# Queries and keys of a head pair: seven half-depth products per two blocks in place of eight

## The chip, the cores and the metric

The kernel runs on one core of one Trainium2 chip. A core has five engines that run side by side, each through its own list of instructions in order: TensorE (matrix products), VectorE and ScalarE (elementwise work), GpSimd, and SyncE, which here issues most of the transfers. The products are written to a small accumulator memory, PSUM, which the kernel divides into banks of 128 x 512 float32; VectorE and ScalarE move results from there to the main on-chip memory, SBUF. The metric is the time of one execution on the device in microseconds; lower is better.

## The reference, cut to what matters

The whole program is four layers on an image x of 512 channels and 64 x 64 pixels: attention, two gated convolution layers and a linear attention, each added to x. The change lies in the first layer. There x is normalized in groups of channels (subtract a mean, multiply by `rstd`, both per group), and then:

```
q = to_tokens(_conv1x1(fmap, wq, gain_in))
k = to_tokens(_conv1x1(fmap, wk, gain_in))
v = to_tokens(_conv1x1(fmap, wv, gain_in))
AA = jnp.sum(q * q, axis=-1)
qk = jnp.einsum('bid,bjd->bij', q, k)
sim = -(AA[:, :, None] + AA[:, None, :] - 2.0 * qk) * scale
attn = jax.nn.softmax(sim, axis=-1)
out = jnp.einsum('bij,bjd->bid', attn, v)
```

There are 8 heads of 64 channels over 4096 pixels. Everything is float32. `_conv1x1` is a product of a 512 x 512 matrix with the 512 x 4096 image.

## The kernel before, in words

The image stays on the chip as `X`: 128 partitions, NC = 4 chunks of channels, N = 4096 pixels, which are cut into NB = 8 blocks of BLK = 512. `_attention_pairs` (from L383) works on two heads at a time, so there are four pairs. For each pair `project` computes the queries Q (kept in the tile `O` of the pair), the keys K, the values V with pixels on the partitions, and the row sums A of the squared queries. Then, for each of the eight query blocks, a loop over 32 key tiles t makes scores (L502), their exponentials on ScalarE (L510, tile `pt`), the running sum of the exponentials on VectorE (L591, L593, tile `acc`), and the product with the values (L520) two tiles later. `close` sums `acc` over the partitions with two small products `ps_d` (L529), takes the reciprocal (L533) and multiplies (L534); the two lines after that (L535, L538) keep a mark of whether the sums were in range. In a pair, `close` of a block is called inside the next block's loop; that of the last block stands before the `project` of the next pair.

`project` first loads the three weight matrices of the pair in one transfer (L438, tile `wqkv`) and multiplies each by `rstd` (`_Centered.scaled`, L357 on ScalarE and L360 on VectorE or GpSimd). In the first pair `_Centered.take` (L349) also subtracts the mean from x block by block on ScalarE while the products run; for later pairs x is already centred, and the weights are loaded and scaled hundreds of microseconds ahead. Then come eight blocks. Each has four products of 128 x 128 by 128 x 512 for Q and four for K (L457), which accumulate the four chunks in a bank, and sixteen products of 128 x 128 by 128 x 128 for V (L468). Q leaves the bank through ScalarE with its scale (L461) and is squared there (L464); K and V leave through VectorE with theirs (L463, L475). After the last block sixteen small products with `halves` (L483) put the sums of squares in one tile `ps_a`, which VectorE turns (L491) and copies into `A` (L492). The exponentials of the pair wait for `A`.

PSUM is divided between the pool `ps_s`, three tiles of two banks, and the two tiles `av0` and `av1` of the values product. In SBUF the pools that matter are `pt` (five tiles of 128 x 1024), `acc` (two tiles of the same size) and `row` (three tiles of 128 x 512, used by `avs` and `rd` when a block closes).

Nobody writes the order of instructions on an engine by hand here, except in the later layers, where `keep_in_program_order` pins TensorE. A planner simulates the program with costs of its own, places each instruction on its engine's list when its operands and a free tile should be ready, and inserts the waits. The order is then fixed: an instruction that waits holds up all that stands behind it on that engine.

The class `_Seven`, further down in the file, is used by the two later layers already. It computes two output matrices (a and b) for two blocks at once. Each matrix is cut in two halves of depth (two chunks each), and the two by two by two half products, which would be eight, are formed as seven products of sums and differences: `sums` makes four combinations of the weights, `differences` four of the blocks, and `steps` holds the seven products p1 to p7 with the additions of their results.

Of the kernel before, what the change touches and what calls it, by code (L numbers as in the profile page):

```python
# [10 lines left out]
FP = mybir.dt.float32  # L11
AF = mybir.ActivationFunctionType
ALU = mybir.AluOpType
# [3 lines left out]
P = 128  # L17
# [46 lines left out]
class _Form:  # L64
# [8 lines left out]
    def __init__(self, run, parts, phy, phx, jy, jx, by, bx, oy, ox):  # L73
        self.run = run
        self.parts, self.phy, self.phx, self.jy, self.jx, self.by, self.bx, self.oy, self.ox = (
            parts, phy, phx, jy, jx, by, bx, oy, ox,
        )
        self.planes = phy * phx
        self.ch = 32 // self.planes
        self.rows, self.w = H // phy, W // phx  # L80
        self.part = self.rows // parts
        self.fh, self.fw = self.rows + jy * by - 1, self.w + jx * bx - 1
        self.plane = self.fh * self.fw
        self.n = self.part * self.w
        self.rounds = BLK // self.n
        self.nr = 16 // self.ch
# [289 lines left out]
            )  # L376

SUM_LOW, SUM_HIGH = 1e-20, 1e30  # L380


def _attention_pairs(tc, a, X, QO, gmask, small, centered, stats, okay):  # L383
# [19 lines left out]
    with tc.tile_pool(name="att1", bufs=1) as p1, tc.tile_pool(  # L403
# [29 lines left out]
        V = p1.tile([P, NT, P], FP, tag="V", name="V")  # L433
        A = p1.tile([P, NT, 2], FP, tag="A", name="A")

        def project(pair):
            w = p1.tile([P, 3, NC, P], FP, tag="wqkv", name=f"wqkv{pair}")
            nc.sync.dma_start(out=w, in_=a["L0_wqkv"][pair])  # L438
            for n in range(3):
                centered.scaled(  # L440
                    w[:, n], rstd, nc.gpsimd if pair else nc.scalar if n else nc.vector
                )
            if pair == 0:
                centered.began()
            Q = QO[pair]
            sq = []
            for b in range(NB):
                cols = ts(b, BLK)
                if pair == 0 and b:
                    for c in range(NC):  # L450
                        centered.take(X[:, c, cols], c)
                if b % 2 == 0:
                    sq.append(ptp.tile([P, 2 * BLK], FP, tag="pt", name="sq"))
                for n in range(2):
                    ps = ps_s.tile([P, 2 * BLK], FP, tag="s", name="ps_qk")[:, 0:BLK]
                    for c in range(NC):
                        nc.tensor.matmul(  # L457
                            ps, w[:, n, c, :], X[:, c, cols], start=(c == 0), stop=(c == NC - 1)
                        )
                    if n == 0:  # L460
                        nc.scalar.activation(Q[:, cols], ps, AF.Copy, scale=2 * scale * gain_in)  # L461
                    else:
                        nc.vector.tensor_scalar(K[:, cols], ps, gain_in, None, ALU.mult)  # L463
                nc.scalar.activation(sq[-1][:, ts(b % 2, BLK)], Q[:, cols], AF.Square)  # L464
                ps = ps_s.tile([P, 2 * BLK], FP, tag="s", name="ps_v")[:, 0:BLK]
                for i in range(QT):
                    for c in range(NC):
                        nc.tensor.matmul(  # L468
                            ps[:, ts(i, P)],
                            X[:, c, ts(b * QT + i, P)],  # L470
                            w[:, 2, c, :],
                            start=(c == 0),
                            stop=(c == NC - 1),
                        )
# [4 lines left out]
            psa = ps_s.tile([P, 2 * BLK], FP, tag="s", name="ps_a")  # L479
            for i in range(4):  # L480
                squares = sq[i].rearrange("p (t j k) -> p j t k", j=4, k=32)
                for j in range(4):
                    nc.tensor.matmul(  # L483
                        psa[ts(j, 32), ts(i, 256)].rearrange("p (t k) -> p t k", k=32),
                        halves,
                        squares[:, j],
                        start=True,
                        stop=True,
                    )
            at = ptp.tile([P, 2 * BLK], FP, tag="pt", name="at")  # L490
            nc.vector.transpose(at, psa)  # L491
            nc.vector.tensor_copy(A, at.rearrange("p (t k) -> p t k", k=32)[:, :, 0:2])  # L492
# [167 lines left out]
class _PlaneConv:  # L660
# [58 lines left out]
    def put(self, i, k, ps, more, bias, step):  # L719


        nc = self.nc
        if more is None:
            self.take(i, k, [ps], lambda d, x: nc.scalar.activation(d, x, AF.Identity, bias=bias))
            return

        def fill(d, x, y):
            if step is None:
                nc.vector.tensor_add(d, x, y)
                return  # L730
            for n in range(self.pair):
                nc.vector.scalar_tensor_tensor(  # L732
                    d[:, n], x[:, n], step, y[:, n], ALU.add, ALU.add
                )

        self.take(i, k, [ps, more], fill)
# [97 lines left out]
                yield  # L834


class _Seven:

    def __init__(self, tc, matmul):
        self.nc, self.matmul = tc.nc, matmul

    def sums(self, eng, a, b, s):

        for out, x, y, op in (
            (s[0], b[:, 0:2], b[:, 2:4], ALU.add),
            (s[1], s[0], a[:, 0:2], ALU.subtract),
            (s[2], a[:, 0:2], b[:, 0:2], ALU.subtract),
            (s[3], a[:, 2:4], s[1], ALU.subtract),
        ):
            eng.tensor_tensor(out, x, y, op)
        return s

    def differences(self, eng, x, t):  # L860

        for j, (a, b) in enumerate(
            (
                (lambda c: x(c, 1), lambda c: x(c, 0)),
                (lambda c: x(2 + c, 1), lambda c: t[0][c]),
                (lambda c: x(2 + c, 1), lambda c: x(c, 1)),
                (lambda c: x(2 + c, 0), lambda c: t[1][c]),
            )
        ):
            for c in range(2):  # L870
                yield eng.tensor_tensor(t[j][c], a(c), b(c), ALU.subtract)

    def steps(self, a, b, s, t, x, bank, keep, put):

        nc = self.nc
        ps, kept = {}, {}

        def add(j, w, hs, first):  # L880

            if first:
                ps[j] = bank(j)
            for c in range(2):
                self.matmul(
                    ps[j], w[:, c], hs[c], start=(first and c == 0), stop=(c == 1),
                    skip_group_check=not first,
                )

        def p1():  # L890
            add(0, a[:, 0:2], [x(c, 0) for c in range(2)], True)
            kept[0] = keep(0, ps[0])

        def p5():
            add(1, s[0], t[0], True)
            kept[1] = keep(1, ps[1])

        def p2():
            add(0, a[:, 2:4], [x(2 + c, 0) for c in range(2)], False)
            put(0, 0, ps[0], None)  # L900

        def p7():
            add(2, s[2], t[2], True)
            nc.vector.tensor_add(kept[1], kept[1], ps[2])

        def p6():
            add(3, s[1], t[1], True)
            nc.vector.tensor_add(kept[0], kept[0], ps[3])

        def p3():  # L910
            add(1, s[3], [x(2 + c, 1) for c in range(2)], False)
            put(0, 1, ps[1], kept[0])

        def p4():
            add(2, b[:, 2:4], t[3], False)
            put(1, 0, ps[2], kept[0])
            put(1, 1, kept[1], kept[0])

        return [p1, p5, p2, p7, p6, p3, p4]


@with_exitstack
def _gated_convs(ctx, tc, a, X, vcol, vall, gmask, small, new_stats, centered, stats, F):

# [12 lines left out]
    for layer in ("L1", "L2"):  # L937
# [65 lines left out]
        def summed(i):  # L1003
            t = [w2p.tile([P, NC, P], FP, tag="w", name="w_sum") for _ in range(2)]
            t = [t[n // 2][:, n % 2 * 2 : n % 2 * 2 + 2] for n in range(4)]
            wsum[i] = seven.sums(nc.vector, w_in[i], w_in[i + 1], t)

        def view(k):
            return lambda c, n: pc.pixels(X[:, c, :], 2 * k + n)
# [149 lines left out]
def _linear_attention(ctx, tc, a, X, vcol, vall, ident, gmask, small, centered, stats, F, Z, out):  # L1159
# [55 lines left out]
    with ExitStack() as st:  # L1215
# [78 lines left out]
        def summed(i):  # L1294
            ss = [kvp.tile([P, BLK], FP, tag="kv", name="w_sum") for _ in range(2)]
            ss = [
                t.rearrange("p (n c m) -> p n c m", n=2, c=2)[:, n] for t in ss for n in range(2)
            ]
            wsum[i] = seven.sums(nc.vector, w_qkv[i], w_qkv[i + 1], ss)

        def differences(k, eng):

# [22 lines left out]
        def bank(j):  # L1325
            return ps_vk.tile([P, BLK], FP, tag=f"vk{j}", name="ps7")
# [191 lines left out]
        def steps(hf, q):  # L1518
            return list(blks[hf, q][2])
# [214 lines left out]
```

## Time and profile before

| what | value |
|---|---|
| three runs | 3900.72, 3907.03, 3908.17 us; median 3907.03 us |
| the profiled execution | 3899.94 us, with a span of 3898.2 us from first to last instruction |
| mean granted TensorE clock of it | 0.995 of full speed |
| attention layer in the span | up to about 2295 us |
| TensorE busy | 3811.4 us, 98% of the span |
| VectorE busy, ScalarE busy | 2509.6 us (64%), 2017.3 us (52%) |
| Q and K products (L457) | 512 rows, 227.2 us busy |
| V products (L468) | 1024 rows, 119.5 us busy |

A row of the groups of instructions reads: line, engine, operation, output<-inputs, tile sizes, number, then busy time and mean nanoseconds of one, then the idle time of the engine before them and what ended it. A row of the timeline reads: start, duration, engine, line, operation, and in brackets an idle time before it. Products on TensorE overlap in their start and end, so their durations can't be added; their starts can be compared. A float32 product of the program is two rows of the trace.

### The profile page before, as it was taken

The page shows a single profiled execution, that of the slowest core. Times are in us where ns is not written, and L with a number is a line of the kernel's source. Part 1 is how long each engine was busy: PE and PEld are TensorE (multiplying, and loading weights), DVE is VectorE, ACT ScalarE, POOL GpSimd, SP SyncE. Part 2 cuts the span into 40 slices and gives each one's busy share as a digit, 9 for nine tenths or more (in the row PEclk, how much of TensorE's full clock was granted, in tenths as well). Part 3 has the DMA queues.
Part 4 walks back from the last instruction along what each step waited for, and adds up shares of the span by engine and source line. Part 5 has one row for each costly group of instructions (what it writes and reads, how often), then busy time and mean ns, then how long its engine had stood idle before and what let it go on. Part 6 is the DMA issues. An engine that isn't in the chain of part 4 may idle for free. (4 is left out here: it accounts for less than half of the span.)

```text
span 3898.2 us, 81595 instructions
## 1 busy us (share of the span) xinstructions
PE 3811.4 (98%) x35526; PEld 1692.3 (43%) x35526; DVE 2509.6 (64%) x2944; ACT 2017.3 (52%) x2909; POOL 109.3 (3%) x94
## 2 busy tenths in 40 slices
PE   6999999999999999999999989999999999999999
PEld 4533335333354333353333335554454544455544
DVE  3577772777736777627776755766657767565435
ACT  3577762777735777626665645552255532354210
POOL 0000000000000000000000000000000000121110
PEclk9999999999999999999999999999999999999999
DMA  2000000000000000000000025562055621463334
GB/s 98 9 2 1 1 1 9 1 1 1 1 1 9 1 1 1 1 9 1 1 1 1 1 73 174 177 191 70 36 172 174 189 66 44 149 174 99 94 93 142
DMA packets 194010, 221.55 MB, mean 57 GB/s; under 512 B 13400, under 2 KB 138584, under 8 KB 193520
## 3 DMA queue, kind: packets, MB, share of 16 engines
q1 hardware_dynamic: 166832, 157.12, 14.5%
q10 hardware_dynamic: 26784, 59.11, 4.1%
q8 instruction: 281, 4.60, 0.5%
q14 instruction: 81, 0.66, 0.1%
q0 software_dynamic: 32, 0.06, 0.0%
HBM read 156.46 MB, written 59.77 MB: 55 GB/s over the span
## 5 line engine op out<-in xcount | busy, mean ns | idle before, releaser
L510 ACT ACTIVATE pt<-ps_s,A 128x512 f32<-128x512 f32 x2048 | 1284.5, 686 | 556.6 <-PE ps_s L502 528.9
L593 DVE TENSOR_TENSOR acc<-acc,pt 128x1024 f32<-128x1024 f32 x960 | 1175.6, 1225 | 331.6 <-ACT pt L510 305.8
L520 PE MATMUL av<-pt,V 64*64 64x512 f32 x8192 | 1112.3, 590 | 0.9 <-ACT pt L510 0.9
L502 PE MATMUL ps_s<-O,K 64*64 64x512 f32 x8192 | 1111.4, 589 | 0.0
L520 PEld LDWEIGHTS av<-pt,V 64*64 64x64 f32 x8192 | 339.6, 133 | 557.5 <-issue 525.7
L502 PEld LDWEIGHTS ps_s<-O,K 64*64 64x64 f32 x8192 | 334.1, 133 | 554.2 <-issue 308.7
L765 ACT COPY S<-S 32x1295 f32<-32x1295 f32 (+1 forms) x272 | 341.3, 1256 | 212.0 <-DMA S<-F 131.8
L687 PEld LDWEIGHTS ps_cv<-S,T 64*32 64x32 f32 x13824 | 191.9, 105 | 109.8 <-issue 72.5
L687 PE MATMUL ps_cv<-S,T 64*32 64x128 f32 x13824 | 230.2, 272 | 4.5 <-DVE S L763 1.8
L687 PE MATMUL ps<-h,w_out_L 128*128 128x512 f32 x512 | 228.7, 599 | 1.5 <-DVE X L1087 1.4
L457 PE MATMUL ps_qk<-X,wqkv 128*128 128x512 f32 x512 | 227.2, 597 | 2.8 <-ACT wqkv L357 2.8
L687 PE MATMUL ps<-diff,w_sum 128*128 128x512 f32 x420 | 197.4, 602 | 0.5 <-issue 0.5
L349 ACT ACTIVATE X<-X,gn_less 128x512 f32<-128x512 f32 x120 | 76.8, 709 | 221.9 <-DVE gn_less L102 210.8
L687 PE MATMUL ps<-X,w_in_L 128*128 128x512 f32 x320 | 152.6, 617 | 12.9 <-ACT kept L1017 5.3
L461 ACT ACTIVATE O<-ps_qk 128x512 f32<-128x512 f32 x32 | 19.1, 596 | 258.2 <-PE ps_qk L457 258.2
L1075 DVE SCALAR_TENSOR_TENSOR h<-ps,vec,h 128x512 f32<-128x512 f32 x112 | 82.5, 748 | 105.7 <-PE ps L687 104.2
L687 PEld LDWEIGHTS ps<-h,w_out_L 128*128 128x128 f32 x512 | 94.3, 190 | 120.2 <-issue 98.7
L687 PE MATMUL ps<-h,pw_L 128*128 128x512 f32 x320 | 144.2, 600 | 1.3 <-DVE plane L732 1.2
L457 PEld LDWEIGHTS ps_qk<-X,wqkv 128*128 128x128 f32 x512 | 95.5, 192 | 113.5 <-issue 109.7
L463 DVE TENSOR_SCALAR K<-ps_qk 128x512 f32<-128x512 f32 x32 | 22.1, 692 | 186.9 <-PE ps_qk L457 186.9
L819 DVE STREAM_TRANSPOSE h<-ps_cv 128x512 f32<-128x512 f32 x112 | 109.4, 1050 | 43.5 <-PE ps_cv L687 42.8
L468 PEld LDWEIGHTS ps_v<-wqkv,X 128*128 128x128 f32 x1024 | 119.4, 192 | 15.3 <-issue 15.3
(161 smaller groups left out, 3074.8 us busy)
## 6 DMA issues: line engine op xcount, KB each, us to landing
T<-in_L_T_dram SPq DMA_DIRECT2D x112, 384.0 KB, 3.7
F<-plane ACTq DMA_DIRECT2D x112, 324.0 KB, 2.9
S<-F SPq DMA_DIRECT2D x224, 162.0 KB, 4.3
row<-G SPq DMA_DIRECT2D x80, 272.0 KB, 3.5
S<-G SPq DMA_DIRECT2D x96, 153.0 KB, 4.3
G<-plane ACTq DMA_DIRECT2D x48, 289.0 KB, 2.2
T<-in_L_T_dram SPq DMA_DIRECT2D x48, 256.0 KB, 3.7
out_dram<-y SPq DMA_DIRECT2D x32, 256.0 KB, 2.0
```

Source lines behind the costliest of these rows:

```text
L349: self.nc.scalar.activation(xs, xs, AF.Identity, bias=less)
L457: nc.tensor.matmul(ps, w[:, n, c, :], X[:, c, cols], start=(c == 0), stop=(c == NC - 1))
L463: nc.vector.tensor_scalar(K[:, cols], ps, gain_in, None, ALU.mult)
L468: nc.tensor.matmul(ps[:, ts(i, P)], X[:, c, ts(b * QT + i, P)], w[:, 2, c, :], start=(c == 0), stop=(c == NC - 1),)
L502: nc.tensor.matmul(ps[ts(half, D), ts(h, BLK)], K[rows, t * P + half * D : t * P + (half + 1) * D], QO[pair][rows, cols], start=True, stop ...
L510: nc.scalar.activation(pt[:, ts(h, BLK)], ps[:, ts(h, BLK)], AF.Exp, bias=A[:, t, h : h + 1])
L520: nc.tensor.matmul(av[half][rows, :], V[keys, t, rows], pt[keys, ts(h, BLK)], start=(t == 0), stop=(t == NT - 1),)
L593: nc.vector.tensor_add(acc, acc, pt)
L687: self.tc.keep_in_program_order(self.nc.tensor.matmul(*args, **kw))
L765: nc.scalar.copy(second, first)
L819: nc.vector.transpose(out, src)
L1075: nc.vector.scalar_tensor_tensor(d, ps, bias, d, ALU.add, ALU.mult)
```

## The change

`_Seven` moves ahead of the attention code, and `sums` becomes a generator that yields after each of its four instructions; the two later layers run it to its end in one go, as they did. `project` uses it for Q (matrix a) and K (matrix b), two blocks k = 0 to 3 at a time.

The scales of Q, K and V, which the evictions applied, go into the weights: a small tile `gains` holds `rstd` times the scale of Q and `rstd` times that of K and V, and `scaled` multiplies the weights by it. Evictions become plain copies and additions. V leaves through ScalarE now. The products p1 and p5 start banks 0 and 1 (`av0`, `av1`), p7 and p6 start banks 2 and 3 (tiles of `ps_s`), and p2, p3, p4 accumulate on top. `keep` copies p1 and p5 to tiles of `row` before that.

The four weight combinations lie in one tile of the pool `acc`, the differences in three tiles of `pt` and one of `acc`, made on VectorE. `ps_a` is allocated at the start of `project`, and the row-sum products of two blocks (`squares`) are called after the first V products of the next two.

```diff
+        gains = p1.tile([P, 2, NC], FP, tag="gains", name="gains")
+        nc.vector.tensor_scalar(gains[:, 0], rstd, 2 * scale * gain_in, None, ALU.mult)
+        nc.vector.tensor_scalar(gains[:, 1], rstd, gain_in, None, ALU.mult)
+        seven = _Seven(tc, nc.tensor.matmul)
...
             for n in range(3):
                 centered.scaled(
-                    w[:, n], rstd, nc.gpsimd if pair else nc.scalar if n else nc.vector
+                    w[:, n], gains[:, min(n, 1)],
+                    nc.gpsimd if pair else nc.scalar if n else nc.vector,
                 )
...
-                for n in range(2):
-                    ps = ps_s.tile([P, 2 * BLK], FP, tag="s", name="ps_qk")[:, 0:BLK]
-                    for c in range(NC):
-                        nc.tensor.matmul(
-                            ps, w[:, n, c, :], X[:, c, cols], start=(c == 0), stop=(c == NC - 1)
-                        )
-                    if n == 0:
-                        nc.scalar.activation(Q[:, cols], ps, AF.Copy, scale=2 * scale * gain_in)
-                    else:
-                        nc.vector.tensor_scalar(K[:, cols], ps, gain_in, None, ALU.mult)
-                nc.scalar.activation(sq[-1][:, ts(b % 2, BLK)], Q[:, cols], AF.Square)
+            psa = ps_s.tile([P, 2 * BLK], FP, tag="s", name="ps_a")
+            wsum = p2.tile([P, 2 * BLK], FP, tag="acc", name="w_sum").rearrange(
+                "p (n c m) -> p n c m", n=4, c=2
+            )
+            wsum = [wsum[:, n] for n in range(4)]
+            sums = seven.sums(nc.vector, w[:, 0], w[:, 1], wsum)
+
+            def differences(k):
+                tiles = [ptp.tile([P, 2 * BLK], FP, tag="pt", name="diff") for _ in range(3)]
+                tiles.append(p2.tile([P, 2 * BLK], FP, tag="acc", name="diff"))
+                t = [[t[:, ts(c, BLK)] for c in range(2)] for t in tiles]
+                return t, seven.differences(
+                    nc.vector, lambda c, n: X[:, c, ts(2 * k + n, BLK)], t
+                )
...
-                nc.vector.tensor_scalar(
-                    V[:, ts(b, QT), :].rearrange("p t d -> p (t d)"), ps, gain_in, None, ALU.mult
-                )
+                nc.scalar.copy(V[:, ts(b, QT), :].rearrange("p t d -> p (t d)"), ps)
+
+            def bank(j):
+                if j < 2:
+                    return ps_av.tile([P, BLK], FP, tag=f"av{j}", name="ps7")
+                return ps_mm.tile([P, BLK], FP, tag="mm", name="ps7")
+
+            def keep(j, ps):
+                t = p3.tile([P, BLK], FP, tag="row", name="kept")
+                nc.scalar.copy(t, ps)
+                return t
...
+                def put(m, n, ps, more):
+                    dst = (K if m else Q)[:, ts(2 * k + n, BLK)]
+                    if more is None:
+                        nc.scalar.copy(dst, ps)
+                    else:
+                        nc.vector.tensor_add(dst, ps, more)
...
+                value(2 * k)
+                if k:
+                    late.pop(0)()
+                for _ in range(4):
+                    next(sums, None)
+                    next(pieces)
+                    next(pieces)
+                for step in steps[:5]:
+                    step()
+                value(2 * k + 1)
+                for step in steps[5:]:
+                    step()
+                sq = ptp.tile([P, 2 * BLK], FP, tag="pt", name="sq")
+                for n in range(2):
+                    nc.scalar.activation(
+                        sq[:, ts(n, BLK)], Q[:, ts(2 * k + n, BLK)], AF.Square
+                    )
+                late.append(lambda k=k, sq=sq: squares(k, sq))
```

The seven products and the additions that they call, unchanged but for their place in the file:

```
        def p1():
            add(0, a[:, 0:2], [x(c, 0) for c in range(2)], True)
            kept[0] = keep(0, ps[0])
        def p5():
            add(1, s[0], t[0], True)
            kept[1] = keep(1, ps[1])
        def p2():
            add(0, a[:, 2:4], [x(2 + c, 0) for c in range(2)], False)
            put(0, 0, ps[0], None)
        def p7():
            add(2, s[2], t[2], True)
            nc.vector.tensor_add(kept[1], kept[1], ps[2])
        def p6():
            add(3, s[1], t[1], True)
            nc.vector.tensor_add(kept[0], kept[0], ps[3])
        def p3():
            add(1, s[3], [x(2 + c, 1) for c in range(2)], False)
            put(0, 1, ps[1], kept[0])
        def p4():
            add(2, b[:, 2:4], t[3], False)
            put(1, 0, ps[2], kept[0])
            put(1, 1, kept[1], kept[0])
        return [p1, p5, p2, p7, p6, p3, p4]
```

More of the change, by code (lines that the diff above doesn't have):

```diff
@@ L376, in _normalize, with __init__, sums, differences @@
             )
+class _Seven:
+    def __init__(self, tc, matmul):
+        self.nc, self.matmul = tc.nc, matmul
+    def sums(self, eng, a, b, s):
+        for out, x, y, op in (
+            (s[0], b[:, 0:2], b[:, 2:4], ALU.add),
+            (s[1], s[0], a[:, 0:2], ALU.subtract),
+            (s[2], a[:, 0:2], b[:, 0:2], ALU.subtract),
+            (s[3], a[:, 2:4], s[1], ALU.subtract),
+        ):
+            yield eng.tensor_tensor(out, x, y, op)
+    def differences(self, eng, x, t):
+        for j, (a, b) in enumerate(
+            (
+                (lambda c: x(c, 1), lambda c: x(c, 0)),
+                (lambda c: x(2 + c, 1), lambda c: t[0][c]),
+                (lambda c: x(2 + c, 1), lambda c: x(c, 1)),
+                (lambda c: x(2 + c, 0), lambda c: t[1][c]),
+            )
+        ):
+            for c in range(2):
+                yield eng.tensor_tensor(t[j][c], a(c), b(c), ALU.subtract)
+    def steps(self, a, b, s, t, x, bank, keep, put):
+        nc = self.nc
+        ps, kept = {}, {}
+        def add(j, w, hs, first):
+            if first:
+                ps[j] = bank(j)
+            for c in range(2):
+                self.matmul(
+                    ps[j], w[:, c], hs[c], start=(first and c == 0), stop=(c == 1),
+                    skip_group_check=not first,
+                )
+        def p1():
+            add(0, a[:, 0:2], [x(c, 0) for c in range(2)], True)
+            kept[0] = keep(0, ps[0])
+        def p5():
+            add(1, s[0], t[0], True)
+            kept[1] = keep(1, ps[1])
+        def p2():
+            add(0, a[:, 2:4], [x(2 + c, 0) for c in range(2)], False)
+            put(0, 0, ps[0], None)
+        def p7():
+            add(2, s[2], t[2], True)
+            nc.vector.tensor_add(kept[1], kept[1], ps[2])
+        def p6():
+            add(3, s[1], t[1], True)
+            nc.vector.tensor_add(kept[0], kept[0], ps[3])
+        def p3():
+            add(1, s[3], [x(2 + c, 1) for c in range(2)], False)
+            put(0, 1, ps[1], kept[0])
+        def p4():
+            add(2, b[:, 2:4], t[3], False)
+            put(1, 0, ps[2], kept[0])
+            put(1, 1, kept[1], kept[0])
+        return [p1, p5, p2, p7, p6, p3, p4]
 SUM_LOW, SUM_HIGH = 1e-20, 1e30
@@ L445, in project, with value @@
             Q = QO[pair]
[L446 to L449, printed above, removed]
-                    for c in range(NC):
-                        centered.take(X[:, c, cols], c)
-                if b % 2 == 0:
-                    sq.append(ptp.tile([P, 2 * BLK], FP, tag="pt", name="sq"))
-                for n in range(2):
-                    ps = ps_s.tile([P, 2 * BLK], FP, tag="s", name="ps_qk")[:, 0:BLK]
-                    for c in range(NC):
-                        nc.tensor.matmul(
-                            ps, w[:, n, c, :], X[:, c, cols], start=(c == 0), stop=(c == NC - 1)
-                        )
-                    if n == 0:
-                        nc.scalar.activation(Q[:, cols], ps, AF.Copy, scale=2 * scale * gain_in)
-                    else:
-                        nc.vector.tensor_scalar(K[:, cols], ps, gain_in, None, ALU.mult)
-                nc.scalar.activation(sq[-1][:, ts(b % 2, BLK)], Q[:, cols], AF.Square)
+            psa = ps_s.tile([P, 2 * BLK], FP, tag="s", name="ps_a")
[10 more added lines that the diff above has]
+                    nc.vector, lambda c, n: X[:, c, ts(2 * k + n, BLK)], t
+                )
+            def value(b):
                 ps = ps_s.tile([P, 2 * BLK], FP, tag="s", name="ps_v")[:, 0:BLK]
@@ L474, in project, with squares @@
                         )
[L475 to L481 removed]
+                nc.scalar.copy(V[:, ts(b, QT), :].rearrange("p t d -> p (t d)"), ps)
[7 more added lines that the diff above has]
+                return t
+            def squares(k, sq):
+                sq = sq.rearrange("p (t j k) -> p j t k", j=4, k=32)
                 for j in range(4):
                     nc.tensor.matmul(
[L484 removed]
+                        psa[ts(j, 32), ts(k, 256)].rearrange("p (t k) -> p t k", k=32),
                         halves,
[L486 removed]
+                        sq[:, j],
                         start=True,
@@ L489, in project @@
                     )
+            late = []
+            for k in range(NB // 2):
+                if pair == 0:
+                    for b in (2 * k, 2 * k + 1):
+                        for c in range(NC if b else 0):
+                            centered.take(X[:, c, ts(b, BLK)], c)
+                def put(m, n, ps, more):
[4 more added lines that the diff above has]
+                        nc.vector.tensor_add(dst, ps, more)
+                t, pieces = differences(k)
+                steps = seven.steps(
+                    w[:, 0], w[:, 1], wsum, t, lambda c, n: X[:, c, ts(2 * k + n, BLK)],
+                    bank, keep, put,
+                )
+                value(2 * k)
[14 more added lines that the diff above has]
+                        sq[:, ts(n, BLK)], Q[:, ts(2 * k + n, BLK)], AF.Square
+                    )
+                late.append(lambda k=k, sq=sq: squares(k, sq))
+            late.pop(0)()
             at = ptp.tile([P, 2 * BLK], FP, tag="pt", name="at")
@@ L834, in conv @@
                 yield
[L837 to L919, printed above, removed]
 @with_exitstack
@@ L1005, in summed @@
             t = [t[n // 2][:, n % 2 * 2 : n % 2 * 2 + 2] for n in range(4)]
-            wsum[i] = seven.sums(nc.vector, w_in[i], w_in[i + 1], t)
+            wsum[i] = t
+            for _ in seven.sums(nc.vector, w_in[i], w_in[i + 1], t):
+                pass
         def view(k):
@@ L1298, in summed @@
             ]
-            wsum[i] = seven.sums(nc.vector, w_qkv[i], w_qkv[i + 1], ss)
+            wsum[i] = ss
+            for _ in seven.sums(nc.vector, w_qkv[i], w_qkv[i + 1], ss):
+                pass
         def differences(k, eng):
```

## The prediction

> **What bounds the kernel now.** I read the page's busy shares first, then who waits for whom on TensorE in the attention stage, then the order of time around one change of head pair. VectorE is DVE in the rows, ScalarE is ACT, TensorE is PE (PEld its weight loads).
>
> ```profile
> PE 3811.4 (98%) x35526; PEld 1692.3 (43%) x35526; DVE 2509.6 (64%) x2944; ACT 2017.3 (52%) x2909; POOL 109.3 (3%) x94
> PEclk9999999999999999999999999999999999999999
> L457 PE MATMUL ps_qk<-X,wqkv 128*128 128x512 f32 x512 | 227.2, 597 | 2.8 <-ACT wqkv L357 2.8
> ```
>
> TensorE is busy in 98% of the span at an undiminished clock. L457 is the line that the change replaces: 4 pairs x 8 blocks x 2 matrices x 4 chunks are 256 products in the program and 512 rows here, so one float32 product is two rows. Its TensorE waited 2.8 us in all.
>
> The waits of TensorE from 0 to 2300 us (engine and line, what it waited for, total, times, longest):
>
> ```profile
> PE gn_ps L100 <- DVE gn_mv L98: 32.9, 2, 27.0
> PE ps_qk L457 <- ACT wqkv L357: 2.8, 1, 2.8
> ...
> PE av L520 <- ACT pt L510: 0.9, 1, 0.9
> PE ps_d L529 <- PE av L520: 0.5, 3, 0.2
> ```
>
> From 32.5 us on, the attention stage stalls for little over 1 us. So a product removed is time removed, and a wait added is time added. Where the second pair begins, in order of time on TensorE (start, duration):
>
> ```profile
> 566.66 2.75 PE L520 MATMUL av<-pt,V 64*64 64x512 f32 x24
> 569.58 1.08 PE L529 MATMUL ps_d<-acc,ones 128*64 128x512 f32 x4 [0.16 <-PE av L520]
> 570.59 7.13 PE L457 MATMUL ps_qk<-X,wqkv 128*128 128x512 f32 x16
> 577.56 3.73 PE L468 MATMUL ps_v<-wqkv,X 128*128 128x128 f32 x32
> 581.13 1.45 PE L457 MATMUL ps_qk<-X,wqkv 128*128 128x512 f32 x3
> ```
>
> The durations of overlapping rows are too long to add up, so I price by starts: a steady block begins every 10.44 us, its V part takes 581.13 - 577.56 = 3.57, which leaves 6.87 for 16 rows: **0.429 us a row**, 0.86 a product.
>
> **Removed.** Two blocks of Q and K take 16 products before and seven pairs, 14, after. That is 2 x 4 x 4 = 32 products or 64 rows: 64 x 0.429 = **27.5 us off**. V (L468) and the row sums (L483) keep their products. In the built instruction streams, everything from the last pair's first score to the end stands in the same order on all five engines; only the start and the four projections change.
>
> **Added on VectorE and ScalarE, under cover.** The later stages already run the same seven products, so the rows are there. On VectorE, at the start of the next stage:
>
> ```profile
> 2298.55 0.17 DVE L122 TENSOR_SCALAR gn_t<-gn_t 128x4 f32<-128x4 f32 x1
> 2299.02 0.69 DVE L871 TENSOR_TENSOR diff<-X 128x512 f32<-128x512 f32 x1 [0.30 <-DMA w_gate_L<-in_L_w_in_dram]
> 2299.63 0.15 DVE L123 TENSOR_TENSOR gn_r<-gn_r,gn_t 128x4 f32<-128x4 f32 x1
> 2299.70 0.68 DVE L871 TENSOR_TENSOR diff<-X 128x512 f32<-128x512 f32 x1
> 2300.30 0.68 DVE L360 TENSOR_TENSOR w_in_L<-w_in_L,gn_r 128x512 f32<-128x512 f32 x1
> ...
> 2302.71 0.41 DVE L857 TENSOR_TENSOR w_sum<-w_in_L 128x256 f32<-128x256 f32 x1
> ```
>
> A difference lasts 0.69 us, but the next instruction starts 0.60 us after it. Two blocks now ask VectorE for 8 differences and 5 additions, 13 x 0.60 = 7.8 us (9.0 at 0.69), against four evictions before, and ScalarE for 5 copies (0.59 each) and 2 squares (0.63): 4.2 us. TensorE needs 20.9 - 1.7 = 19.2 us for them. There is room; were it gone, the surplus would count 16 times. The four weight sums (0.42 each) come 1.7 us once a pair; for pairs 2 to 4 they go after the closing work of the block before, where VectorE already runs behind. That backlog holds exp tiles, of which there are five: at 529.14 an exp takes a tile freed at about 525.9, so 3 us of room hides 1.7. No DMA is added or moved past another; the weights of the next pair still load 500 us early, and the GpSimd scaling stays where it was.
>
> Inside a pair of blocks I followed each wait. The second product reuses a bank that ScalarE copies out: 0.20 to start (K's eviction at 577.76 after 577.56), 0.58, 0.14 back to TensorE (569.44 to 569.58) = 0.92, under a product pair of 1.72. In the middle groups V's bank is freed by `kept[0] += ps3`, which stands on VectorE behind `kept[1] += ps2` and two differences: with product seven ending at 0, the addition starts at about 2.0, ends at 2.7, reaches TensorE at 2.83; TensorE arrives after p6 and p3, at 3.44. Room 0.6 us.
>
> **Added on the path.** Four costs, from the order in which the built kernel issues.
>
> (a) Start. VectorE now does two differences and two small gains ahead of the first scaled weight, and a third just before it. The first two wait for centred x, the third ScalarE centring being done at 32.5.
>
> ```profile
> 31.31 0.17 DVE L122 TENSOR_SCALAR gn_t<-gn_t 128x4 f32<-128x4 f32 x1
> 31.51 0.16 DVE L123 TENSOR_TENSOR gn_r<-gn_r,gn_t 128x4 f32<-128x4 f32 x1
> 31.71 0.69 DVE L360 TENSOR_TENSOR wqkv<-wqkv,gn_r 128x512 f32<-128x512 f32 x1
> ```
>
> L360 started at 31.71. Three differences at 0.60 and two gains at about 0.06 put it at 33.6: **1.9 us** later (2.4 at full durations and dependent gains). ScalarE's weight scaling moves by 1.3 and stays ahead, as TensorE is still in p1.
>
> (b) Change of pair, three times. VectorE's order becomes: second-last addition to `acc`, three differences, last addition. Before:
>
> ```profile
> 566.49 1.23 DVE L593 TENSOR_TENSOR acc<-acc,pt 128x1024 f32<-128x1024 f32 x1 [0.49 <-ACT pt L510]
> 568.21 1.23 DVE L593 TENSOR_TENSOR acc<-acc,pt 128x1024 f32<-128x1024 f32 x1 [0.49 <-ACT pt L510]
> 570.09 0.69 DVE L599 TENSOR_TENSOR avs<-avs,av 128x512 f32<-128x512 f32 x1 [0.66 <-ACT avs L596]
> ```
>
> The last addition ended at 569.44 and TensorE's ps_d product began at 569.58, 0.16 after it was free: this chain was already the last to end. With the differences at 567.62, 568.22 and 568.83 it starts at 569.43, 1.22 later, and all TensorE work of the new pair stands behind ps_d. 3 x 1.22 = **3.7 us**. Here a rule of the Trainium skill weighs against the row: "VectorE: DVE Perf Modes", section "The DRAIN you can't avoid", has the next instruction start only once the pipe is empty, which makes each difference its full 0.69 and the delay 3 x 0.69 - 0.49 + 0.07 = 1.6, 4.9 in all. The page excepts instructions that are not held; the 0.60 spacing above is such a case, so I take 3.7 and keep 4.9.
>
> (c) End of a projection, four times. In the last pair of blocks V comes after only one product of p3 (0.86 of cover), and its bank needs 0.20 + 0.69 + 0.14 = 1.03: 0.17 each, 0.7. Then the row sums are turned: before, the transpose started 0.14 after its products; now K's last eviction (0.69) stands in front, and exp starts about 0.25 later, with scores filling three buffers meanwhile: 0.2 each, 0.8. Together **1.5 us** (0 to 3).
>
> (d) The row-sum products now come in four bursts a pair in place of one; V to L483 showed a gap of 0.09 (654.21 to 654.30), so 12 x 0.09 = **1.1 us** (0 to 2).
>
> Sum: 27.5 - 1.9 - 3.7 - 1.5 - 1.1 = **19.3 us saved**; with all costs at their high ends 27.5 - 12.3 = 15.2, with none 27.5. The second rule I weighed: "TensorE: Matmul & The Clock Gate", section "What's actually happening": an idle window of about 3.4 us halves the clock for about as long. It speaks against (b), whose gaps grow from 0.16 to 1.4 us. The trace shows the price once: the first 16 rows of L457 took 8.70 us (32.50 to 41.20) in place of 6.87, 1.8 lost. By the rule 1.4 is too short, and I count nothing; if it did happen, 3 x 1.8 = 5.5 more.
>
> The profiled execution took 3899.94 us around a span of 3898.2, so its successor should show a span near 3879. The median of the runs is 3907.03, 7 above it; the difference carries over: 3907.0 - 19.3 = **3887.7 us**.
>
> **Rivals.**
> First, the waits find cover that I do not see (the differences run while VectorE was idle anyway, 0.49 us per step): the gain is 25 to 27.5, 3879.5 to 3882. For it: VectorE is only 64% busy. Against it: at the pair change the row shows no room, and order on an engine is fixed.
>
> Second, the eviction chain binds in the groups with differences between the two additions (12 of 16). Room is 0.6 us; if the additions that read PSUM or the waits between engines come 1.2 us later than the rows say, 0.6 x 12 = 7.2 us more: 3894.9. For it: ScalarE centres x in the first pair with 24 instructions that stand among its first copies, where I find only 0.4 us of room. Against it: the next stage runs the same chain with a TensorE that seldom waits.
>
> Third, slower: the same chain, late by more. It decides at 19.3 / 12 = 1.6 us of stall per group, 2.2 us beyond my times, say because the differences wait for slots that the products have not freed. At 3 us beyond, 12 x 2.4 = 28.8 lost: 9.5 slower, 3916.5. Against it: the slots of the next group's differences are freed some 5 us before their use.
>
> That the products are not fewer is no rival: the built kernel holds 32 less.
>
> **How the numbers follow.** My forecast 0.72, with its own range 3882 to 3893; first rival 0.11; second 0.12, to 3899; slower 0.05. A difference of 0.2%, 7.8 us, is about what this measurement can tell from none, so faster means under 3899.2, and slower over 3914.8. Faster takes the first two and nearly all of the second rival: 0.88 after moving some to the edge; same 0.07; slower 0.05. Range 3877 to 3898: it covers the first rival, whose low end falls with a run like the lowest of the three (3900.72), and most of the second.
>
> **What would show it.** Two-row products of the seven (the line of `_Seven`'s products) 448 in attention in place of 512. First of them near 34.4 us. ps_d at the pair changes starting 1.2 us after TensorE is free, waiting for VectorE. A steady pair of blocks every 19.2 to 19.3 us. V's last product group waiting 0.17. Wrong would be: TensorE waits of over 0.3 us inside the groups, ps_d without a wait, or a clock row that dips after the pair changes.

## The result, and the profile after

The changed kernel takes 3884.6 us (median of five runs, 3878.84 to 3887.82), the kernel before 3906.72 (five runs, the three of above among them, 3900.72 to 3908.17): a ratio of 0.9944, with a 95% interval of 0.993 to 0.9959. The forecast was 3887.7, in a range of 3877 to 3898. The profiled execution took 3884.6 us, with a span of 3882.9; its forecast was a span near 3879.

From the page of the changed kernel, the lines that answer to those shown of before:

```profile
PE 3789.8 (98%) x35462; PEld 1682.9 (43%) x35462; DVE 2605.4 (67%) x3106; ACT 2046.6 (53%) x2957; POOL 111.3 (3%) x94
PEclk9999999999999999999999999999999999999999
```

TensorE has 64 rows fewer (35526 to 35462), VectorE 162 instructions more. The products of `_Seven` in attention, by their tiles, from the view of their line (the three times are least, median and greatest duration in ns):

```profile
L427 PE MATMUL ps<-diff,w_sum x192: 592/592/593, 41.3 to 1700.7; 128*128 128x512 f32 x192
L427 PE MATMUL ps<-X,wqkv x128: 592/592/1193, 34.5 to 1697.3; 128*128 128x512 f32 x128
L427 PE MATMUL ps<-X,w_sum x64: 592/592/595, 51.7 to 1706.2; 128*128 128x512 f32 x64
L427 PE MATMUL ps<-diff,wqkv x64: 592/592/595, 53.4 to 1707.9; 128*128 128x512 f32 x64
```

That is 448 in place of 512. Who TensorE waited for in the attention stage (total, times, longest):

```profile
PE ps L427 <- issue: 4.5, 1, 4.5
...
PE ps_d L666 <- DVE acc L730: 4.2, 3, 1.4
...
PE av L657 <- ACT pt L647: 0.9, 1, 0.9
```

The first wait was 2.8 us before and is now 4.5; the three waits of ps_d were 0.5 and are 4.2. Inside the groups of two blocks the view lists none. One delay leaves no idle time there, since the rows overlap; it stands in the last group of a pair, here in order of time:

```profile
639.91 1.02 PE L427 MATMUL ps<-X,w_sum 128*128 128x512 f32 x2
640.11 0.69 DVE L450 TENSOR_TENSOR kept<-kept,ps 128x512 f32<-128x512 f32 x1 [0.97 <-PE ps L427]
640.85 3.84 PE L558 MATMUL ps_v<-wqkv,X 128*128 128x128 f32 x32
644.53 1.02 PE L427 MATMUL ps<-X,w_sum 128*128 128x512 f32 x2
```

Two rows of p3 fill 0.86, to 640.77; V starts 0.08 later, 0.05 after the addition that frees its bank, and its 32 rows take 3.68 in place of 3.57. Together that is 0.19 us a pair.

The change of pair, first TensorE, then VectorE, in order of time:

```profile
562.71 2.75 PE L657 MATMUL av<-pt,V 64*64 64x512 f32 x24
566.86 1.08 PE L666 MATMUL ps_d<-acc,ones 128*64 128x512 f32 x4 [1.39 <-DVE acc L730]
567.87 3.84 PE L558 MATMUL ps_v<-wqkv,X 128*128 128x128 f32 x32
```

```profile
562.54 1.23 DVE L730 TENSOR_TENSOR acc<-acc,pt 128x1024 f32<-128x1024 f32 x1 [0.49 <-ACT pt L647]
563.68 1.29 DVE L413 TENSOR_TENSOR diff<-X 128x512 f32<-128x512 f32 x2
564.89 0.69 DVE L413 TENSOR_TENSOR diff<-X,diff 128x512 f32<-128x512 f32 x1
565.49 1.22 DVE L730 TENSOR_TENSOR acc<-acc,pt 128x1024 f32<-128x1024 f32 x1
```

Three differences stand between the last two additions to `acc`; ps_d starts 1.39 us after TensorE is free. A middle group of two blocks on TensorE, p1 at 591.37, p3 at 600.05, V, p4, V, and the next row sums at 610.73:

```profile
590.80 0.64 PE L581 MATMUL ps_a<-sq,halves 128*32 128x256 f32 x8
591.37 1.99 PE L427 MATMUL ps<-X,wqkv 128*128 128x512 f32 x4
593.19 1.88 PE L427 MATMUL ps<-diff,w_sum 128*128 128x512 f32 x4
594.90 1.88 PE L427 MATMUL ps<-X,wqkv 128*128 128x512 f32 x4
596.62 3.60 PE L427 MATMUL ps<-diff,w_sum 128*128 128x512 f32 x8
600.05 1.88 PE L427 MATMUL ps<-X,w_sum 128*128 128x512 f32 x4
601.77 3.73 PE L558 MATMUL ps_v<-wqkv,X 128*128 128x128 f32 x32
```

The products start 1.72 us apart, but for two places: the row sums take 0.57 (590.80 to 591.37), not the 0.47 that a quarter of the former burst would (1.87 for 32 rows), and p1 behind them 1.82.

Where the time went can be read from three stretches of each profile. The table gives, for one execution each, the start of the first product of the first pair, that pair's stretch from its first product to its first score, the length of the same stretch in pairs 2 and 4, and the start of the fourth pair's first score, all in us. (In the kernel before the stretch of a pair begins with Q and K, after with V.)

| kernel | first product | pair 1 | pair 2 | pair 4 | first score of pair 4 |
|---|---|---|---|---|---|
| before | 32.50 | 87.31 | 85.58 | 85.58 | 1726.44 |
| after | 34.47 | 81.30 | 79.90 | 79.90 | 1709.03 |
| scales only | 32.92 | 87.44 | 85.58 | 85.57 | 1726.89 |
| differences after the sum | 34.21 | 82.12 | 79.90 | 79.90 | 1705.93 |
| start (differences after the first weight) | 32.96 | 82.49 | 79.91 | 79.90 | 1708.72 |
| one burst | 34.34 | 80.77 | 78.72 | 79.90 | 1705.92 |
| longer chain | 34.39 | 82.66 | 79.71 | 79.71 | 1709.73 |
| longer chain, order held | 34.51 | 85.92 | 84.25 | 84.24 | 1726.72 |
| all three repairs | 32.87 | 80.36 | 78.71 | 79.91 | 1700.36 |

From before to after the last column falls by 17.4 us. From there to the end the two kernels have the same instructions in the same order, and that stretch took 2171.8 us before and 2173.9 after, and between 2167.5 (one burst) and 2174.2 in the others. So single executions differ by several us for reasons outside the change, and the small repairs below are read from these stretches, not from whole times. The granted clock goes with it: of the changed kernel's five runs the two at a mean clock of 0.995 took 3878.84 and 3880.84 us, and the three at 0.994 took 3884.6 to 3887.82.

### The profile page after: what moved, and what is told of

It reads as the page before. It is cut to its first block, busy times and chain, and to the rows that moved or that the text cites. A ratio compares the mean times of both kernels' runs of the same rounds, so it can differ in the third digit from the quotient of the medians.

```text
span 3882.9 us, 81692 instructions
## 1 busy us (share of the span) xinstructions
PE 3789.8 (98%) x35462; PEld 1682.9 (43%) x35462; DVE 2605.4 (67%) x3106; ACT 2046.6 (53%) x2957; POOL 111.3 (3%) x94
## 3 DMA queue, kind: packets, MB, share of 16 engines
q1 hardware_dynamic: 166832, 157.12, 14.9%
## 5 line engine op out<-in xcount | busy, mean ns | idle before, releaser
L413 DVE TENSOR_TENSOR diff<-X 128x512 f32<-128x512 f32 x176 | 117.3, 684 | 63.3 <-PE ps L824 40.0
L413 DVE TENSOR_TENSOR diff<-X,diff 128x512 f32<-128x512 f32 x176 | 117.6, 682 | 7.7 <-PE ps L824 4.3
L824 PE MATMUL vkp<-kT,vT 128*128 128x512 f32 x256 | 117.1, 601 | 4.7 <-DVE vT L1500 4.7
L558 PE MATMUL ps_v<-wqkv,X 128*128 128x128 f32 x1024 | 120.7, 276 | 0.0
```

The lines of the kernel that those rows point to most:

```text
L558: nc.tensor.matmul(ps[:, ts(i, P)], X[:, c, ts(b * QT + i, P)], w[:, 2, c, :], start=(c == 0), stop=(c == NC - 1),)
L824: self.tc.keep_in_program_order(self.nc.tensor.matmul(*args, **kw))
```

## The experiments

**The scales alone.** The kernel before, with the gains folded into the weights, plain evictions, and V through ScalarE; eight products.

```diff
-                    w[:, n], rstd, nc.gpsimd if pair else nc.scalar if n else nc.vector
+                    w[:, n], gains[:, min(n, 1)],
+                    nc.gpsimd if pair else nc.scalar if n else nc.vector,
...
-                        nc.scalar.activation(Q[:, cols], ps, AF.Copy, scale=2 * scale * gain_in)
+                        nc.scalar.copy(Q[:, cols], ps)
...
-                        nc.vector.tensor_scalar(K[:, cols], ps, gain_in, None, ALU.mult)
+                        nc.vector.tensor_copy(K[:, cols], ps)
...
-                nc.vector.tensor_scalar(
-                    V[:, ts(b, QT), :].rearrange("p t d -> p (t d)"), ps, gain_in, None, ALU.mult
-                )
+                nc.scalar.copy(V[:, ts(b, QT), :].rearrange("p t d -> p (t d)"), ps)
```

> The kernel before with the scales folded into the weights and V leaving through ScalarE, but eight products as they were: one part of the change alone. My theory (the time lies in TensorE's products): 512 rows of the Q and K products stay, two small instructions of 0.07 us stand ahead of the first scaled weight, so the first product starts about 0.15 us later and nothing else moves; time the same as before within 0.1%. Rival (the plain evictions and the move of V to ScalarE carry part of the gain): the stretch of a projection gets shorter, 3 us or more in all.

Measured: 3902.93 against 3904.05 us, a ratio of 0.9996 (0.9987 to 1.0005). The stretches of pairs 2 and 4 are 85.58 and 85.57, as before. The first product stands at 32.92, 0.42 later than in the kernel before, where 0.15 was expected; 0.22 of it is the input's (the first gn_ps product, which takes the mean of the groups, at 27.24 against 27.02). This part of the change is worth nothing by itself; the rival falls.

**The differences behind the last addition.** The changed kernel, with a planner's edge that keeps the differences of a pair's first two blocks behind the last addition to `acc` of the pair before.

```diff
-                            nc.vector.tensor_add(acc, acc, pt)
+                            last = nc.vector.tensor_add(acc, acc, pt)
...
+            def behind(k):
+                if k or last is None:
+                    return nullcontext()
+                return tc.issue_after(last.ins)
...
-                    next(pieces)
-                    next(pieces)
+                    with behind(k):
+                        next(pieces)
+                        next(pieces)
```

> The changed kernel with the differences of a pair's first two blocks issued on VectorE behind the last addition to acc of the pair before. My theory: the three waits of ps_d, 4.2 us together, fall to the 0.5 us of the kernel before, the second product of the pair still finds its differences ready (they are done some 3 us before TensorE gets there), and the last score of the attention stands 3.7 us nearer to the first product. Rival (the wait only changes its place): TensorE waits as long for the differences at the pair's p5 or p7, and less than 1 us is won.

Measured: one run, 3881.85 us. Its waits of TensorE in attention:

```profile
PE ps L427 <- issue: 4.5, 1, 4.5
PE av L663 <- ACT pt L653: 0.9, 1, 0.9
PE ps_d L672 <- PE av L663: 0.5, 3, 0.2
```

ps_d is back at the 0.5 us of before, no other wait has come, and the stretches of pairs 2 and 4 are unchanged at 79.90. The second pair's first product follows the first pair's first score after 450.88 us (116.33 to 567.21), against 452.10 (115.77 to 567.87) in the changed kernel: 1.22 us, three times. The wait was there for the order on VectorE alone.

**The differences behind the first scaled weight.** The changed kernel with the same edge (`behind(k)` around the differences, as in the diff above) in the first pair alone, to the instruction that scales the query weights.

```diff
+            if pair == 0:
+                last = nc.vector.tensor_tensor(
+                    w[:, 0], w[:, 0],
+                    gains[:, 0].unsqueeze(2).to_broadcast([P, NC, P]), ALU.mult,
+                )
```

> The changed kernel with the first pair's differences of the first two blocks issued on VectorE behind the first scaled weight. My theory: the weight is scaled at about 32.1 us after the same start of the input and the first product stands at about 33.0 in place of 34.5 us, 1.5 us won; p5 does not wait, as it comes 6 us after the first product. Rival: the first product comes earlier but p5 or the V products wait for the same time, since ScalarE's scaling and centring set the pace of the first two blocks; nothing won by the first score.

Measured: one run, 3883.3 us. The first product stands at 32.96, 1.51 us earlier than in the changed kernel, as expected, and no wait shows at p5. But the first score is at 115.45, only 0.32 earlier: the stretch has grown from 81.30 to 82.49. The V rows of the first block show where. The start of the changed kernel:

```profile
34.47 2.05 PE L427 MATMUL ps<-X,wqkv 128*128 128x512 f32 x2 [4.49 <-issue]
36.31 4.25 PE L558 MATMUL ps_v<-wqkv,X 128*128 128x128 f32 x32
40.40 1.02 PE L427 MATMUL ps<-X,wqkv 128*128 128x512 f32 x2
```

And that of this one:

```profile
32.96 2.05 PE L427 MATMUL ps<-X,wqkv 128*128 128x512 f32 x2 [3.00 <-ACT X L349]
34.80 5.44 PE L563 MATMUL ps_v<-wqkv,X 128*128 128x128 f32 x32
40.08 1.02 PE L427 MATMUL ps<-X,wqkv 128*128 128x512 f32 x2
```

The same 32 rows take 4.09 us from start to start in the one, 5.28 in the other, and 3.57 later on. TensorE runs slowly at first, for a time that differs from execution to execution (last section); in this one it took back most of what the earlier start had won. I count the 1.5 us as shown for the start of the first product, and as not shown for the time.

**One burst of row sums.** The changed kernel; in the first three pairs the squares go to the query tile of the next pair, which is not in use yet, and all sixteen row-sum products come at the end of the projection.

```diff
-                if k:
+                if k and pair == HEADS // 2 - 1:
                     late.pop(0)()
...
+                if pair < HEADS // 2 - 1:
+                    sq = QO[pair + 1][:, ts(k, 2 * BLK)]
+                else:
+                    sq = ptp.tile([P, 2 * BLK], FP, tag="pt", name="sq")
...
-            late.pop(0)()
+            if pair < HEADS // 2 - 1:
+                psa = ps_s.tile([P, 2 * BLK], FP, tag="s", name="ps_a")
+            for f in late:
+                f()
```

> The changed kernel with the row-sum products of the first three pairs in one burst at the end again (the squares lie in the next pair's unused query tile); the fourth pair keeps its four bursts. If a burst costs what the rows of the changed kernel show, 0.29 us (0.09 ahead, 0.10 within, 0.10 behind), the stretch from a pair's first V product to its first score falls from 79.9 to about 79.0 us in pairs 2 and 3 and stays in pair 4; 2.6 us in all. If it costs the 0.09 that I had predicted: 0.3 us a pair, 0.8 in all.

Measured: one run, 3875.59 us. The stretches of pairs 2 and 3 fall from 79.90 to 78.72 (both), and that of pair 4 stays at 79.90. So the edit is worth 1.18 us a pair, more than either number expected; 78.72 is 6.86 below the 85.58 of before, just what eight products fewer come to (16 rows of 0.429). Whatever else the change cost in the projection of a pair is gone with this edit. (Of the 9.0 us by which this run is shorter than the changed kernel's median, only 3.1 lie ahead of the fourth pair's first score.) The end of the second pair's projection, in this kernel and in the changed one:

```profile
642.16 1.88 PE L427 MATMUL ps<-diff,wqkv 128*128 128x512 f32 x4
643.97 1.93 PE L580 MATMUL ps_a<-O,halves 128*32 128x256 f32 x32
645.84 2.38 PE L647 MATMUL ps_s<-O,K 64*64 64x512 f32 x20
```

```profile
645.39 1.88 PE L427 MATMUL ps<-diff,wqkv 128*128 128x512 f32 x4
647.20 0.64 PE L581 MATMUL ps_a<-sq,halves 128*32 128x256 f32 x8
647.77 1.52 PE L639 MATMUL ps_s<-O,K 64*64 64x512 f32 x12
```

32 rows in one burst take 1.87 us, four times eight take 4 x 0.57 = 2.28; 0.41 of the 1.18. The 0.09 ahead of a burst comes three times less (0.27), and so does the 0.10 of the p1 behind it (0.30). That makes 0.98. The repair also gives V a third buffer, and V in the last group then comes ahead of p3, at 636.87, with no delay: the 0.19 shown above is gone too, 1.17 in all. The next kernel parts the two: it keeps the four bursts, but V in its last group is on time, and its pairs take 79.71, 0.19 less than the changed kernel and 0.99 more than this one. So three bursts cost 0.99, 0.33 each.

**A longer chain.** The changed kernel, with the addition that frees the bank of p6 followed by a subtraction and an addition of the same bank.

```diff
             nc.vector.tensor_add(kept[0], kept[0], ps[3])
+            if slow:
+                nc.vector.tensor_sub(kept[0], kept[0], ps[3])
+                nc.vector.tensor_add(kept[0], kept[0], ps[3])
```

> The changed kernel with the addition that frees the bank of p6 (kept[0] += ps3) followed by a subtraction and an addition of the same bank, so that the bank comes free some 3.0 us later in the two middle groups of a pair (differences stand between) and 1.5 us later in the last. My theory (the chain has 0.6 us of room in the middle groups and none in the last): V waits 2.4 us in 8 groups and 1.6 in 4, some 25 us in all, and the gain of the change is gone. Rival (the chain already binds): 3.0 in 8 and 1.6 in 4, over 30 us. Second rival (the bank is not on the path): no change.

Measured: 3884.77 against 3902.68 us, a ratio of 0.995 (0.9935 to 0.9965): no slower than the changed kernel (3884.6), and no new wait. My expectation was wrong, and the profile shows why: in this kernel the planner has placed p4, and one product of the next p1, ahead of V, from 602.96 on, so that V comes at 605.53, when its bank is free (the third operation runs from 603.99 to 604.67). The experiment had changed the order that it meant to test. So I held the order.

**The longer chain, order held.** The same three operations, with p4 and the next two blocks' products tied behind this group's second V.

```diff
+                gate = tc.issue_after(odd.ins) if k else nullcontext()
...
-                value(2 * k + 1)
-                for step in steps[5:]:
-                    step()
+                odd = value(2 * k + 1)
+                steps[5]()
+                with tc.issue_after(odd.ins):
+                    steps[6]()
```

> As e5 (the bank of p6 freed by three operations in place of one), but with TensorE's order held as in the changed kernel: p4 and the next two blocks' products behind the V products of this group, so that the planner cannot put other products into the gap. My theory (the chain is on the path and has some 0.55 us of room): the rows of e5 have the bank free at 604.8 where V would come at 602.96, so V waits 1.9 us in the 8 middle groups and about 0.8 in the 4 last ones, 18 us in all, and the time goes back to within 5 us of the kernel before. Rival (the bank is not what V waits for): no wait, time as the changed kernel.

Measured: 3899.84 against 3902.15 us, a ratio of 0.9993 (0.9984 to 1.0001). The gain is gone. TensorE's waits from 30 to 2240 us, and VectorE and TensorE in a middle group:

```profile
PE ps_v L561 <- DVE kept L453: 14.9, 12, 1.6
PE ps L427 <- issue: 4.5, 1, 4.5
PE ps_d L674 <- DVE acc L738: 4.2, 3, 1.4
```

```profile
604.63 1.88 PE L427 MATMUL ps<-X,w_sum 128*128 128x512 f32 x4
604.98 0.68 DVE L450 TENSOR_TENSOR kept<-kept,ps 128x512 f32<-128x512 f32 x1
...
607.38 0.68 DVE L453 TENSOR_TENSOR kept<-kept,ps 128x512 f32<-128x512 f32 x1
608.11 3.84 PE L561 MATMUL ps_v<-wqkv,X 128*128 128x128 f32 x32 [1.60 <-DVE kept L453]
```

V waits twelve times for the bank, 14.9 us together; I had expected 18. The chain is on the path. In the changed kernel its addition runs from 600.40 to 601.08, and V starts at 601.77, so with the 0.05 that the last line shows between such an addition's end (608.06) and V (608.11) there are 0.6 us of room. No run holds the order without the longer chain, but the rows of the second pair leave nothing for the order alone. V is due 1.72 after the start of p3; it comes 1.76, 1.78 and 0.67 later (at 608.11, 629.93 and 650.63), and each time its 32 rows take 0.11 more (3.68 for 3.57). That is 4.5 us, less the 0.19 that the last group of the changed kernel loses already, and the stretch has grown by just this, 4.35.

**All three repairs.** The three edits above together: the edge ahead of the differences in all four pairs (to the first scaled weight in the first, to the last addition in the others), and one burst of row sums in the first three.

```diff
+            if pair == 0:
+                last = nc.vector.tensor_tensor(
...
+                    with behind(k):
...
+                if pair < HEADS // 2 - 1:
+                    sq = QO[pair + 1][:, ts(k, 2 * BLK)]
...
+            for f in late:
+                f()
...
+                            last = nc.vector.tensor_add(acc, acc, pt)
```

> The changed kernel with all three repairs: differences behind the last addition at the changes of pair, behind the first scaled weight at the start, row sums of three pairs in one burst. My theory: 3.7 + 1.5 + 2.6 = 7.8 us less than the changed kernel, about 3877 us where that takes 3884.6, some 0.75% under the kernel before. Rival (the three share one cover, so that a repair brings out another wait): 3 us or less.

Measured: 3874.04 us (five runs, 3873.24 to 3876.44) against 3902.68, a ratio of 0.9923 (0.991 to 0.9937): the best of all. The first score of the fourth pair stands at 1700.36, 8.7 us before that of the changed kernel, against the 7.8 expected. Its waits in the attention stage are 3.0 us for the first product, 0.9 and 0.5.

## Why the prediction was right

**The gain is the removed products.** 64 rows at 0.429 us were to be 27.5 us. With one burst of row sums the stretches of pairs 2 and 3 are 6.86 shorter than before; four times that is 27.4. The scales alone gave nothing.

**(a) Start, 1.9 us.** The first product was forecast near 34.4 and stands at 34.47. The mean of the groups came 0.29 later in this execution, though (the first gn_ps product at 27.31 against 27.02), so the cost is 1.7: the two gains started 0.07 apart and the differences 0.60.

**(b) Change of pair, 3.7 us.** Waits of 4.2 in place of 0.5: 3.7, the number itself, and moving three instructions on VectorE took it away. By the rule that the prediction weighed (the Trainium skill, "VectorE: DVE Perf Modes", section "The DRAIN you can't avoid") it would have been 4.9. In the lines above the differences begin at 563.68 and 564.89, two spacings of 0.60, and the addition 0.60 after that: the row decides, as I took it. The gap of 1.39 us did not bring the slow clock back, in keeping with the window of about 3.4 us in the Trainium skill ("TensorE: Matmul & The Clock Gate", section "What's actually happening"): V's 32 rows after it take 3.67, the same as behind the gap of 0.16 with the differences after the sum (567.21 to 570.88).

**(c) and (d), the terms that were mis-sized.** The two together were 2.6 us and measured 4.8: 85.58 - 6.87 - 79.90 leaves 1.19 a pair. Of (c), V's part is right: 0.19 a pair for its bank, against 0.17. The exponentials did not come later at all: K's last eviction (647.30, 0.69) overlaps the transpose (647.91), since VectorE starts the next instruction 0.61 us after it, and exp starts 1.71 us after the first score (647.77 to 649.48), as before (656.17 to 657.88). So (c) is 0.8 in place of 1.5. And (d) was sized by one gap, 0.09 for each of twelve further bursts: 1.1 us. The three bursts fewer of the one-burst kernel show 0.33 each, some 4.0 in all; a burst of eight rows costs more than a quarter of 32, and the next product is late too. This is the step of the forecast that failed: it priced a burst by the gap ahead of it alone. The 0.7 too much in (c) made up for only part of the 2.9 too little in (d).

**The sum and the medians.** The costs come to 1.7 + 3.7 + 4.8 = 10.2 us where 8.2 were forecast, which leaves 17.3 of the 27.5: 17.4 are read at the fourth pair's first score, where the first pair's slow start was 0.3 us shorter than before and the input 0.3 later. The forecast was 19.3. That the median came within 3.1 us of its forecast is in part luck. The medians lie 22.1 us apart and the two profiled spans 15.3, for the rest of the kernel differs by a few us from run to run; and in three later sets of runs the kernel before had medians of 3902.15 to 3904.05, not 3906.72.

**The period of a group** was to be 19.2 to 19.3 us and is 19.93 (590.80 to 610.73). There I had left out the row sums' own 0.47; the rest is what a burst costs beyond its rows, 0.29.

**The rivals.** The first, all waits covered, is refuted by the ps_d rows. The second and third, the chain through VectorE to V's bank, were not there in the changed kernel; its room was reckoned at 0.6 us and read at 0.6. The third rival's mechanism is real: in the held order 14.9 us of such waits brought the kernel back to the time of before. But it needs the order held, since the planner moved other products into the gap by itself when it saw the longer chain; I had not thought of that.

## What to carry to other kernels

When one engine is full, price an edit by the start-to-start time of that engine's rows, and then follow, instruction by instruction, what the new order puts in front of each thing that the full engine waits for: here three small instructions on an engine with room to spare cost 3.7 us by their place alone. Work of a second shape that is cut into small bursts on TensorE costs at each burst, ahead, within and behind (here 0.33 us in all); count the bursts. And when a kernel is planned by a scheduler, an experiment that lengthens a chain must hold the order too, or it tests another order.

## What the runs showed of the hardware that was not expected

**The slow start is not of one length.** From the first product to p5 there are four rows of 0.429 us and 32 of V in 3.57, 5.3 us at full speed. It took 6.8 in the changed kernel, 7.0 with all repairs (32.87 to 39.91), 7.6 with the differences after the sum (34.21 to 41.82), 8.0 in the start kernel and 8.3 with the longer chain (34.39 to 42.73), with no wait in between: 1.5 to 3.0 us lost, as much as the start repair could win or more. Row by row, V starts every 0.21 us at first and then, from one row to the next, every 0.11: even steps, as no wait would leave them. The wide steps end at 37.38 in the changed kernel, at 38.22 in the start kernel and at 40.50 with the longer chain, which is 2.9, 5.3 and 6.1 us after the first product. The Trainium skill ("TensorE: Matmul & The Clock Gate", section "What's actually happening") has a free-running window of about 3.4 us, whose phase varies; the low end lies near it, and the high end is longer. The granted clock does not show it here. The windows view of the changed kernel (stretch, length, then busy time and count of PE, PEld, DVE, ACT, POOL, clock, DMA share, GB/s):

```profile
34.00:36.00 2.00, 1.53 (x2) 0.84 (x3) 2.00 (x6) 2.00 (x7) 0.00 (x0) 1.00 0.00 0
36.00:38.00 2.00, 2.00 (x12) 1.69 (x11) 2.00 (x4) 2.00 (x4) 0.00 (x0) 1.00 0.00 0
38.00:40.00 2.00, 2.00 (x20) 2.00 (x20) 1.41 (x3) 2.00 (x5) 0.00 (x0) 1.00 0.00 0
```

The clock reads 1.00 in each, while 11 rows of V start in the second stretch and 18 in the third (the counts of the view hold those that began before).
